# Spreading the spectrum interleave over two phases of the Fourier mixing stage of a two-layer preactivation network

## The chip, the cores and the metric

The kernel runs on one core of a Trainium2 chip. The metric is the device time of one execution in microseconds (us). All data is float32. The engines are named as the profile names them: PE is the matrix engine and PEld its weight load, DVE the vector engine, ACT the scalar engine, POOL the general-purpose engine, SP the engine whose queue issues most of the loads.

## The reference

Input is `x` of 16 images x 16 channels x 256 x 256. Layer 0 normalises `x` in groups and adds a Laplace neural operator; layer 1 is a block of small convolutions, also on a normalised input. Only layer 0's spectral part is touched here:

```python
alpha = jnp.fft.fft2(x, axes=(-2, -1))
A = 1.0 / (omega1[:, None, None, None] - weights_pole1[None])
Bm = 1.0 / (omega2[:, None, None, None] - weights_pole2[None])
S = jnp.einsum('ikpq,oikp,xikq->oxik', weights_residue, A, Bm)
output_residue1 = jnp.einsum('biox,oxik->bkox', alpha, S)
...
x1 = jnp.fft.ifft2(output_residue1, s=(Ny, Nx), axes=(-2, -1)).real
```

For every frequency pair (o, x) a 16 x 16 complex matrix `S[o, x]` over channels is built and multiplied with the spectrum `alpha` of all 16 images; then the inverse transform runs back. Because the input is real, only about half of the o frequencies are computed.

## The kernel before

`forward` runs four stages one after the other: `layer0_forward` (normalisation, forward transform, tables; it leaves the spectrum in the HBM tensor `al`), `layer0_mix` (the stage of this change), `layer0_back` (inverse transform along y, residual) and `layer1`. Inside `layer0_mix` the order of the instructions of PE, ACT, DVE and POOL is the order of the program text (`manual_schedule`); each engine runs its own list in order, and semaphores make it wait where data or buffers need it. The DMAs that SP issues are placed by the scheduler, and SP issues them in that order.

The stage works on 33 groups of four o frequencies (`NF = 33`). For each group g there are two phases.

The **S phase** builds the matrices `S` for group g+1. `residues` (matmuls on line 659) makes eight PSUM tiles per group, two per step f = 0..3; each is copied into the SBUF tile `s` by ACT (line 670) or DVE (line 668). Between them `turn` (line 694) transposes the products `y` of group g, eight transposes per f, each half copied to a tile `yt` by DVE (line 700) and ACT (line 698).

The **mixing phase** has four steps f. Each runs `columns` (line 713), the inverse transform along x of a quarter of the group before, whose two PSUM tiles `ph` are read by ACT (`anti`, line 723) and DVE (`w`, lines 726 and 727) and turned into two tiles `h` by DVE and POOL, which POOL writes to HBM; and then `mix` (line 678), 64 matmul calls of `S` with the spectrum, whose PSUM tile `pg` ACT copies into `y` (line 771).

The spectrum comes to `mix` in three moves. `load_spectrum` (line 607, on SP) loads a piece `alc` of two images, 256 KB; a group has eight pieces, and there are two buffers, so that piece n+2 can be loaded only when piece n has been read. `interleave` copies a piece into the tile `alx` with the image index innermost: DVE copies the even pieces (line 626) and ACT the odd ones (line 624), and it issues the next load. `place` (line 632, on SP) copies `alx` with four DMAs of 512 KB into `alb`, a block-diagonal tile that is zero elsewhere; it can start only when the last `mix` of the group has read the old `alb`.

There is one buffer each of `alx`, `alb`, `y`, `s` and `lt`; two PSUM buffers (tag `pg`) shared by `residues` and `mix`; two each of `pt` and `ph`; four of `yt`; three of `h`. In the text below the eight pieces of a group are called piece 0 to piece 7, and the steps S0 to S3 and M0 to M3. Before the change the pieces are interleaved two per step in M0 to M3, behind the `columns` of the step and ahead of its `y` copy:

```python
ps = mix(s, y, 16 * f)
if more:
    for q in (2 * f, 2 * f + 1):
        interleave(alx, q)
nc.scalar.copy(y[:, :, 16 * f : 16 * f + 16], ps.rearrange("p x j -> p j x"))
```

At the head of the stage `alb` is cleared first, half on DVE and half on POOL (lines 593 and 594), then all eight pieces of group 0 go through the two `alc` buffers, then comes the first S phase, and then the loop over the groups.

Of the kernel before, what the change touches and what calls it, by code (L numbers as in the profile page):

```python
# [10 lines left out]
F32 = mybir.dt.float32  # L11
# [7 lines left out]
C = 16  # L19
N = 256  # L20
G = 8
P = 128
NF = 33
# [542 lines left out]
def layer0_mix(ctx, tc, d, al, hd, tabs):  # L566
# [3 lines left out]
    nc = tc.nc  # L570
    nb = d["x"].shape[0]
# [5 lines left out]
    def load_poles(g):  # L577
        av = ap.tile([P, 32, 4, 3], F32, tag="av", name="av")
        nc.sync.dma_start(out=av.rearrange("p k f l -> p (k f l)"), in_=avd[g])
        return av  # L580

    av = load_poles(0)
# [7 lines left out]


    alb = cp.tile([P, 4, N, nb], F32, name="alb")
    nc.vector.memset(alb[:, :2], 0.0)
    nc.gpsimd.memset(alb[:, 2:], 0.0)

    lp = ctx.enter_context(tc.tile_pool(name="ml", bufs=1))
    gp = ctx.enter_context(tc.tile_pool(name="mg", bufs=1))
    hp = ctx.enter_context(tc.tile_pool(name="mh", bufs=3))
# [4 lines left out]
    def load_spectrum(g, q):  # L603

        t = gp.tile([P, 2, N], F32, tag="alc", name="alc", bufs=2)
        src = al[g // 4 * 2 + g % 2, :, :, :, 2 * q : 2 * q + 2, g % 4 // 2]
        nc.sync.dma_start(out=t, in_=src.rearrange("h v c b x -> (h v c) b x"))
        return t

    wanted = ((g, q) for g in range(NF) for q in range(nb // 2))  # L610
    spectrum = []

    def load_next():

        following = next(wanted, None)
        if following:
            spectrum.append(load_spectrum(*following))

    def interleave(alx, q):

        dst = alx[:, :, 2 * q : 2 * q + 2]
        src = spectrum.pop(0).rearrange("p b x -> p x b")
        if q % 2:
            nc.scalar.copy(dst, src)
        else:
            nc.vector.tensor_copy(dst, src)
        load_next()

    def place(alx):

        for f in range(4):
            nc.sync.dma_start(
                out=alb[f::4, f].rearrange("p x b -> p (x b)"),
                in_=alx[f::4].rearrange("p x b -> p (x b)"),
            )

    def poles(av):


        lt = lp.tile([P, 32, 3, 4, 4], F32, tag="lt", name="lt")  # L640
        shape = [P, 32, 4, 4]
        for plane in range(3):
            nc.vector.tensor_tensor(
                lt[:, :, plane],
                av[:, :, :, plane].unsqueeze(2).to_broadcast(shape),
                m16.unsqueeze(1).unsqueeze(3).to_broadcast(shape),
                ALU.mult,
            )
        return lt.rearrange("p (k g) l c f -> p k g l (c f)", g=4)
# [22 lines left out]
    def mix(s, y, x0):  # L672

        ps = psg.tile([P, 16, 64], F32, tag="pg", name="pg")
        for x in range(16):
            for q in range(4):
                i = 4 * (x0 + x) + q
                nc.tensor.matmul(  # L678
                    ps[32 * q : 32 * q + 32, x],
                    lhsT=s[:, i].rearrange("p v k -> p (v k)"),  # L680
                    rhs=alb[:, :, N // 2 * (i % 2) + i // 2],
                    start=True,
                    stop=True,
                )
        return ps

    def turn(y, f):

        yt = hp.tile([P, 8, 8, C], F32, tag="yt", name="yt", bufs=4)
        for t0 in range(0, 8, 4):  # L690
            pt = pst.tile([P, 4, P], F32, tag="pt", name="pt")
            for t in range(4):
                j = 16 * f + 2 * (t0 + t)
                nc.tensor.transpose(pt[:, t], y[:, j : j + 2].rearrange("p q x -> p (q x)"), ident)  # L694
            dst = yt[:, :, t0 : t0 + 4].rearrange("p c t k -> p t c k")
            src = pt.rearrange("p t (c k) -> p t c k", k=C)
            if t0:
                nc.scalar.copy(dst, src)
            else:
                nc.vector.tensor_copy(dst, src)  # L700
        return yt

    def columns(g, f, yt):

        ph = [psh.tile([P, 2, 4, 64], F32, tag="ph", name="ph") for q in range(2)]
        for e in range(2):
            for v in range(2):
                blocks = slice(0, 4, 3) if v == 0 else slice(1, 3)
                for c in range(2):
                    i = 2 * (2 * c + e) + v  # L710
                    for q in range(2):
                        lanes = slice(64 * q, 64 * q + 64)
                        nc.tensor.matmul(  # L713
                            ph[q][:, e, blocks],
                            lhsT=yt[lanes, i].rearrange("p t k -> p (t k)"),
                            rhs=ix[lanes, i].rearrange("p (b x) -> p b x", b=2),
                            start=c == 0,
                            stop=c == 1,
                        )
        ws = []  # L720
        for q in range(2):
            anti = hp.tile([P, 2, 2, 64], F32, tag="anti", name="anti", bufs=2)
            nc.scalar.copy(anti, ph[q][:, :, 2:])
            w = hp.tile([P, 2, 2, 2, 64], F32, tag="w", name="w", bufs=2)
            sym = ph[q][:, :, :2]
            nc.vector.tensor_tensor(w[:, 0], sym, anti, ALU.add)
            nc.vector.tensor_tensor(w[:, 1, :, :, ::-1], sym, anti, ALU.subtract)  # L727
            ws.append(w)
        for q, w in enumerate(ws):
            o = hp.tile([P, 2, 4, 64], F32, tag="h", name="h", bufs=3)  # L730
            parts = o.rearrange("p v s x -> p s v x")
            nc.vector.tensor_tensor(parts[:, 0::3], w[:, :, 0], w[:, :, 1], ALU.add)
            nc.gpsimd.tensor_tensor(parts[:, 2:0:-1], w[:, :, 0], w[:, :, 1], ALU.subtract)  # L733
            o = o.rearrange("p v s x -> p v (s x)")
            fy = 4 * g + 2 * (f % 2) + f // 2
            if fy % P:
                nc.gpsimd.dma_start(
                    out=hd[fy % 2, :, fy % P // 2, q].rearrange("v b k x -> (b k) v x"), in_=o
                )
            else:  # L740
                nc.gpsimd.dma_start(
                    out=hd[0, fy // P, 0, q].rearrange("b k x -> (b k) x"), in_=o[:, 0]
                )

    E = mybir.EngineType
    with tc.manual_schedule(engines={E.PE, E.Activation, E.DVE, E.Pool}):
        load_next()
        load_next()
        lt = poles(av)
        av = load_poles(1)  # L750
        alx = gp.tile([P, N, nb], F32, tag="alx", name="alx")
        for q in range(nb // 2):
            interleave(alx, q)
        place(alx)
        s = gp.tile([P, N, 2, C], F32, tag="s", name="s")
        for k0 in range(0, C, 2):
            residues(lt, s, k0)
        yts = []
        for g in range(NF):
            more = g + 1 < NF  # L760
            if more:
                alx = gp.tile([P, N, nb], F32, tag="alx", name="alx")
            y = gp.tile([P, 64, 64], F32, tag="y", name="y")
            for f in range(4):
                if g:
                    columns(g - 1, f, yts[f])
                ps = mix(s, y, 16 * f)
                if more:
                    for q in (2 * f, 2 * f + 1):
                        interleave(alx, q)  # L770
                nc.scalar.copy(y[:, :, 16 * f : 16 * f + 16], ps.rearrange("p x j -> p j x"))  # L771
                if more and f == 1:
                    lt = poles(av)
                    if g + 2 < NF:
                        av = load_poles(g + 2)
            yts = []
            if more:
                place(alx)
                s = gp.tile([P, N, 2, C], F32, tag="s", name="s")
                for f in range(4):  # L780
                    for k0 in (4 * f, 4 * f + 2):
                        residues(lt, s, k0)
                    yts.append(turn(y, f))
            else:
                columns(g, 0, turn(y, 0))

# [780 lines left out]
```

## Time and profile before

| what | us |
|---|---|
| median of three runs (lowest, highest) | 6735.75 (6724.75, 6745.13) |
| the profiled execution, its own time | 6730.94 |
| its span in the profile | 6729.2 |
| the mixing stage, first clearing of `alb` to the last `mix` | 1380.0 to about 2556 |
| first `mix` of group 0 | 1420.4 |
| PE busy over the whole span | 6169.1 (92%) |

The span is the stretch from the first to the last instruction in the profile; the profiled execution took 1.7 us more, and was 4.8 us below the median. The stage covers some 17% of the span. A time such as 2087.15 in a line of the profile is a start in us from the span's beginning; the next number is the length. In square brackets stands how long the engine was idle just before, and what ended that idle time; "issue" there means that no semaphore in the profile ended it.

### The profile page before, as it was taken

How to read it: one execution, taken by the hardware profiler on the slowest of the kernel's cores; microseconds unless marked ns; L12 is line 12 of the kernel's file. 1: busy time of each engine (PE TensorE's matmuls, PEld its weight loads, DVE VectorE, ACT ScalarE, POOL GpSimd, SP SyncE). 2: the span in 40 equal slices, each digit the busy share in tenths (PEclk: the TensorE clock that was granted, in tenths of full speed). 3: DMA queues.
4: the chain of work that ended last, by engine and by line, in shares of the span. 5: the costliest groups of instructions: out<-in, count | busy, mean ns of one | idle time of the engine just before them, and what ended most of it. 6: DMA issues, size and time to landing. Idle time of an engine off the chain costs nothing.

```text
span 6729.2 us, 153347 instructions
## 1 busy us (share of the span) xinstructions
PE 6169.1 (92%) x59944; PEld 3412.2 (51%) x59944; DVE 5290.3 (79%) x10118; ACT 3410.0 (51%) x5666; POOL 3531.3 (52%) x4619
## 2 busy tenths in 40 slices
PE   6989989978888888999799999999999999999996
PEld 5777777856777666777233333333333333333331
DVE  8988997535655556888788888888888888888885
ACT  1223333334444442222666666666666666666661
POOL 2334444433333335666556566665667656666563
PEclk9999999989999999999899999999999999999998
DMA  3333433355555558999688888988898888998886
GB/s 98 122 121 124 124 105 118 101 195 188 188 184 189 195 179 279 327 327 316 194 247 256 259 274 268 297 244 265 270 286 277 257 275 268 282 278 258 270 275 213
DMA packets 752372, 1512.38 MB, mean 225 GB/s; under 512 B 82858, under 2 KB 572646, under 8 KB 705286
## 3 DMA queue, kind: packets, MB, share of 16 engines
q1 hardware_dynamic: 623910, 1028.46, 49.3%
q0 software_dynamic: 127744, 474.12, 21.0%
q8 instruction: 478, 7.83, 0.5%
q14 instruction: 240, 1.97, 0.1%
HBM read 876.59 MB, written 556.47 MB: 213 GB/s over the span
## 4 chain that ended last, share of the span: by engine, by line
PE 68%; DVE 16%; DMA 6%; ACT 5%; issue 3%; POOL 1%; SPq 0%; ACTq 0%; DVEq 0%; POOLq 0%
PE c2ps L1207 17%; PE c L1059 14%; PE pd L1127 13%; PE ps L659 4%; PE ph L713 3%; DMA alc<-al 3%; ACT wide L1107 3%; PE pg L678 2%; PE px L313 2%; PE pt L694 2%; DVE u L224 2%; PE py L882 2%; PE pu L207 2%; PE pr L1086 2%; PE py L883 2%
## 5 line engine op out<-in xcount | busy, mean ns | idle before, releaser
L1107 ACT ACTIVATE wide<-c,b 32x512 f32<-32x512 f32 x2176 | 1477.5, 679 | 312.5 <-PE c L1059 264.0
L1138 DVE TENSOR_TENSOR top<-pd,t 32x512 f32<-32x512 f32 x2176 | 1503.9, 691 | 53.9 <-DMA cf<-top 1.3
L1059 PE MATMUL c<-z,w 102*128 102x512 f32 x2048 | 1002.0, 621 | 109.1 <-ACT wide L1107 89.0
L1119 POOL COPY wide<-wide 32x1031 f32<-32x1031 f32 (+1 forms) x576 | 578.6, 1004 | 877.8 <-ACT wide L1107 850.7
L1135 DVE TENSOR_TENSOR t<-pd,r 64x512 f32<-64x512 f32 x1088 | 743.7, 684 | 357.9 <-PE pd L1127 297.0
L1127 PE MATMUL pd<-wide,dw 128*128 128x512 f32 x2048 | 993.9, 607 | 14.8 <-DVE top L1138 11.0
L1207 PE MATMUL c2ps<-rows,c 128*32 128x512 f32 x6144 | 722.9, 603 | 6.3 <-DVE odd L1234 4.8
L1059 PEld LDWEIGHTS c<-z,w 102*128 102x128 f32 x2048 | 373.0, 193 | 697.0 <-issue 462.1
L1127 PEld LDWEIGHTS pd<-wide,dw 128*128 128x128 f32 x2048 | 382.4, 193 | 576.2 <-issue 419.4
L1120 POOL COPY wide<-wide 32x1031 f32<-32x1031 f32 (+1 forms) x576 | 576.8, 1001 | 33.5
L1078 ACT ACTIVATE bot<-c,b 128x512 f32<-128x512 f32 x544 | 344.0, 683 | 468.2 <-issue 384.1
L733 POOL TENSOR_TENSOR h<-w 128x256 f32<-128x256 f32 x258 | 191.5, 742 | 638.4 <-DVE w L727 630.6
L313 PE MATMUL px<-wxn,u 128*64 128x256 f32 x4224 | 481.5, 379 | 4.0 <-ACT o L320 4.0
L207 PE MATMUL pu<-fy,eo 128*128 128x128 f32 x2048 | 432.1, 295 | 48.5 <-DVE u L224 43.9
L1207 PEld LDWEIGHTS c2ps<-rows,c 128*32 128x32 f32 x6144 | 176.9, 109 | 515.6 <-issue 404.3
L895 POOL TENSOR_TENSOR x<-x,o 128x512 f32<-128x512 f32 x256 | 324.0, 1266 | 215.4 <-DVE o L894 215.3
L214 PE MATMUL pv<-at,eo 128*128 128x128 f32 x2048 | 419.4, 288 | 0.0
L313 PEld LDWEIGHTS px<-wxn,u 128*64 128x64 f32 x4224 | 309.1, 137 | 155.2 <-ACT o L320 8.4
L320 ACT ACTIVATE o<-px,rsc 128x512 f32<-128x512 f32 (+1 forms) x272 | 186.1, 686 | 389.2 <-PE px L313 355.5
L194 POOL TENSOR_TENSOR eo<-z 128x1024 f32<-128x1024 f32 x64 | 154.3, 2411 | 401.5 <-PE pv L214 380.9
L207 PEld LDWEIGHTS pu<-fy,eo 128*128 128x128 f32 x2048 | 334.7, 206 | 53.8 <-issue 42.1
L659 PE MATMUL ps<-tt,lt 64*32 64x256 f32 x8448 | 290.8, 402 | 75.6 <-ACT y L771 35.9
(226 smaller groups left out, 11234.7 us busy)
## 6 DMA issues: line engine op xcount, KB each, us to landing
rows<-cf SPq DMA_DIRECT2D x128, 2176.0 KB
z<-zn SPq DMA_DIRECT2D x768, 257.8 KB
cf<-top POOLq DMA_DIRECT2D x512, 240.0 KB, 6.8
cf<-bot POOLq DMA_DIRECT2D x96, 840.0 KB, 11.2
alc<-al SPq DMA_DIRECT2D x264, 256.0 KB
alb<-alx SPq DMA_DIRECT2D x132, 512.0 KB
zn<-zb SPq DMA_DIRECT2D x128, 516.0 KB
o<-zn SPq DMA_DIRECT2D x128, 516.0 KB
```

The lines of the kernel that those rows point to most:

```text
L207: nc.tensor.matmul(pu[:, xh, :, e], lhsT=lhs, rhs=fy[:, e].rearrange("p (v m) -> p v m", v=2), start=True, stop=True,)
L214: nc.tensor.matmul(pv[:, a, xh], lhsT=lhs, rhs=at[:, e, ch].rearrange("p l m -> p (l m)"), start=e == 0, stop=e == 1,)
L313: nc.tensor.matmul(ps[64 * k : 64 * k + 64, :, h], lhsT=u[:, h, part, g0 + j + k].rearrange("p c f g -> p (c f g)"), rhs=wxn[:, h, part], ...
L659: nc.tensor.matmul(ps[32 * g : 32 * g + 32, odd, v], lhsT=lt[lanes, kk, g, 1 - v : 3 - v].rearrange("p l c -> p (l c)"), rhs=tt[lanes, kk, g],
L1059: nc.tensor.matmul(ps[:, a], lhsT=w, rhs=z[:k, c : c + 2, 0:N], start=True, stop=True)
L1107: nc.scalar.activation(self.feat[64 - 32 * q : 96 - 32 * q, f, self.groups[g], :H], ps[q][32 * f : 32 * f + 32], AF.Mish, bias=b1[0][32 * ...
L1119: nc.gpsimd.tensor_copy(flat[0:32, f, 1:m], flat[64:96, f, 0 : m - 1])
L1120: nc.gpsimd.tensor_copy(flat[96:128, f, 0 : m - 1], flat[32:64, f, 1:m])
L1127: nc.tensor.matmul(ps, lhsT=dwt if self.tail else dw, rhs=self.feat[:, f, cs, :H], start=True, stop=True,)
L1135: nc.vector.tensor_tensor(t[64:128], ps[:64], self.r[:, cs], ALU.mult)
L1138: nc.vector.tensor_tensor(self.top[32 * f : 32 * f + 32, cs, q], ps[lanes], t[lanes], ALU.add)
L1207: nc.tensor.matmul(ps[32 * j : 32 * j + 32], lhsT=w[:, blk], rhs=src[:, 4 * j + blk : 4 * j + blk + 4, x : x + H], start=(i, blk) == (0, 0 ...
```

## The change

Four things are done in `layer0_mix`, and one of them at its head.

1. Pieces 0 to 3 of the next group but one are interleaved in the S phase, two each behind the `residues` and `turn` of S2 and the `residues` of S3; pieces 4 to 7 follow in M0 and M1. M2 and M3 have none. The tile `alx` is therefore taken directly after `place` has read the one before.
2. `turn(y, 3)` leaves S3 and stands behind the first `columns` of the next mixing phase, ahead of `mix`.
3. The `y` copy of M3 is written as two halves of 512 columns, the first on ACT and the second on DVE.
4. Group 0's spectrum is loaded by four DMAs of 512 KB into the four `yt` buffers, which are not yet in use; its copies into `alx` come after the first S phase's `residues`. DVE clears its half of `alb` after `poles` and not before it.

```diff
+    def load_first(q):
+        t = hp.tile([P, 8, 8, C], F32, tag="yt", name="first", bufs=4)
+        view = t.rearrange("p t k c -> p (t k c)").rearrange("p (b x) -> p b x", x=N)
+        src = al[0, :, :, :, 4 * q : 4 * q + 4, 0]
+        nc.sync.dma_start(out=view, in_=src.rearrange("h v c b x -> (h v c) b x"))
+        return view
...
-    wanted = ((g, q) for g in range(NF) for q in range(nb // 2))
+    wanted = ((g, q) for g in range(1, NF) for q in range(nb // 2))
...
+        first = [load_first(q) for q in range(nb // 4)]
+        nc.gpsimd.memset(alb[:, 2:], 0.0)
+        lt = poles(av)
+        nc.vector.memset(alb[:, :2], 0.0)
+        av = load_poles(1)
         load_next()
         load_next()
-        lt = poles(av)
-        av = load_poles(1)
-        alx = gp.tile([P, N, nb], F32, tag="alx", name="alx")
-        for q in range(nb // 2):
-            interleave(alx, q)
-        place(alx)
         s = gp.tile([P, N, 2, C], F32, tag="s", name="s")
         for k0 in range(0, C, 2):
             residues(lt, s, k0)
-        yts = []
+        alx = new_spectrum()
+        for q, piece in enumerate(first):
+            copy = nc.scalar.copy if q % 2 else nc.vector.tensor_copy
+            copy(alx[:, :, 4 * q : 4 * q + 4], piece.rearrange("p b x -> p x b"))
+        place(alx)
+        alx = new_spectrum()
+        for q in range(4):
+            interleave(alx, q)
+        yts, last = [], None
         for g in range(NF):
             more = g + 1 < NF
...
             for f in range(4):
                 if g:
                     columns(g - 1, f, yts[f])
+                    if f == 0:
+                        yts.append(turn(last, 3))
+                if f == 0:
+                    y = gp.tile([P, 64, 64], F32, tag="y", name="y")
                 ps = mix(s, y, 16 * f)
-                if more:
-                    for q in (2 * f, 2 * f + 1):
+                if more and f < 2:
+                    for q in (4 + 2 * f, 5 + 2 * f):
                         interleave(alx, q)
-                nc.scalar.copy(y[:, :, 16 * f : 16 * f + 16], ps.rearrange("p x j -> p j x"))
+                dst, src = y[:, :, 16 * f : 16 * f + 16], ps.rearrange("p x j -> p j x")
+                if f < 3:
+                    nc.scalar.copy(dst, src)
+                else:
+                    nc.scalar.copy(dst[:, :32], src[:, :32])
+                    nc.vector.tensor_copy(dst[:, 32:], src[:, 32:])
...
             if more:
                 place(alx)
                 s = gp.tile([P, N, 2, C], F32, tag="s", name="s")
+                if g + 2 < NF:
+                    alx = new_spectrum()
                 for f in range(4):
                     for k0 in (4 * f, 4 * f + 2):
                         residues(lt, s, k0)
-                    yts.append(turn(y, f))
+                    if f < 3:
+                        yts.append(turn(y, f))
+                    if f >= 2 and g + 2 < NF:
+                        for q in (2 * f - 4, 2 * f - 3):
+                            interleave(alx, q)
```

More of the change, by code (lines that the diff above doesn't have):

```diff
@@ L592, in layer0_mix @@
     alb = cp.tile([P, 4, N, nb], F32, name="alb")
-    nc.vector.memset(alb[:, :2], 0.0)
-    nc.gpsimd.memset(alb[:, 2:], 0.0)
     lp = ctx.enter_context(tc.tile_pool(name="ml", bufs=1))
@@ L617, in load_next, with new_spectrum @@
             spectrum.append(load_spectrum(*following))
+    def new_spectrum():
+        return gp.tile([P, N, nb], F32, tag="alx", name="alx")
     def interleave(alx, q):
@@ L757, in layer0_mix @@
             residues(lt, s, k0)
-        yts = []
+        alx = new_spectrum()
[7 more added lines that the diff above has]
+        yts, last = [], None
         for g in range(NF):
             more = g + 1 < NF
-            if more:
-                alx = gp.tile([P, N, nb], F32, tag="alx", name="alx")
-            y = gp.tile([P, 64, 64], F32, tag="y", name="y")
             for f in range(4):
@@ L766, in layer0_mix @@
                     columns(g - 1, f, yts[f])
+                    if f == 0:
+                        yts.append(turn(last, 3))
+                if f == 0:
+                    y = gp.tile([P, 64, 64], F32, tag="y", name="y")
                 ps = mix(s, y, 16 * f)
-                if more:
-                    for q in (2 * f, 2 * f + 1):
+                if more and f < 2:
+                    for q in (4 + 2 * f, 5 + 2 * f):
                         interleave(alx, q)
-                nc.scalar.copy(y[:, :, 16 * f : 16 * f + 16], ps.rearrange("p x j -> p j x"))
+                dst, src = y[:, :, 16 * f : 16 * f + 16], ps.rearrange("p x j -> p j x")
[4 more added lines that the diff above has]
+                    nc.vector.tensor_copy(dst[:, 32:], src[:, 32:])
                 if more and f == 1:
@@ L775, in layer0_mix @@
                         av = load_poles(g + 2)
-            yts = []
+            yts, last = [], y
             if more:
```

## The prediction

> **What bounds the stage now.** I read the page first (PE 92% busy over the span, so a stage that leaves PE idle is where time can be won), then the stretches inside the mixing stage, then the waits in it, then one group in order of time.
>
> From the table of stretches, PE, PEld, DVE, ACT, POOL in turn, then PE's clock, the DMA share and GB/s:
>
> ```profile
> 1452.00:2554.00 1102.00, 954.90 (x29210) 769.62 (x29210) 644.64 (x1227) 488.05 (x752) 372.16 (x508) 0.95 0.56 187
> 2072.00:2074.00 2.00, 2.00 (x48) 1.31 (x40) 1.29 (x2) 1.23 (x2) 0.00 (x0) 1.00 0.83 289
> 2074.00:2076.00 2.00, 2.00 (x61) 1.38 (x46) 0.91 (x2) 1.28 (x2) 0.00 (x0) 1.00 0.08 25
> 2076.00:2078.00 2.00, 2.00 (x31) 1.83 (x31) 1.44 (x2) 0.58 (x1) 0.00 (x0) 1.00 0.00 0
> ```
>
> No engine is full: PE 87%, DVE 58%, ACT 44%. The DMA engines, at 56%, fall to nothing from 2074 to about 2082, late in the S phase. A group's first `y` copy starts at 1452.03 in group 1 and at 2504.68 in group 31, so an inner group takes (2504.68 - 1452.03) / 30 = 35.1 us. PE's own work in one is 27.3 us: four `mix` of 1.93 (2078.45 to 2080.38), four `columns` of 1.98, four S steps of 2.91 (the distance of their transposes). So 7.8 us a group are lost. The waits between 1430 and 2556, who <- whom, sum, times, longest:
>
> ```profile
> ACT alx L624 <- DMA alc<-al: 257.6, 90, 4.7
> PEld ps L659 <- ACT y L771: 50.3, 28, 3.5
> PE pg L678 <- issue: 59.5, 55, 2.8
> PE ph L713 <- issue: 34.7, 23, 2.5
> PE ps L659 <- ACT y L771: 35.9, 17, 3.0
> PE ps L659 <- issue: 10.5, 5, 2.7
> ```
>
> ACT waits 258 us for the spectrum's pieces, and PE's only large semaphore wait is for ACT's `y` copy. One group shows how the two hang together, ACT and then PE:
>
> ```profile
> 2079.13 0.76 ACT L624 COPY alx<-alc 128x512 f32<-128x512 f32 x1
> 2087.15 0.74 ACT L624 COPY alx<-alc 128x512 f32<-128x512 f32 x1 [3.97 <-DMA alc<-al]
> 2092.80 0.75 ACT L624 COPY alx<-alc 128x512 f32<-128x512 f32 x1 [1.43 <-DMA alc<-al]
> 2098.17 0.74 ACT L624 COPY alx<-alc 128x512 f32<-128x512 f32 x1 [2.76 <-DMA alc<-al]
> 2098.82 1.00 ACT L771 COPY y<-pg 128x1024 f32<-128x1024 f32 x1
> ...
> 2086.80 0.41 PE L678 MATMUL pg<-alb,s 128*32 128x64 f32 x11 [2.37 <-issue]
> 2099.87 0.45 PE L659 MATMUL ps<-tt,lt 64*32 64x256 f32 x8 [1.77 <-ACT y L771]
> ```
>
> Pieces 1, 3, 5, 7 end 8.0, 5.6 and 5.4 us apart, because each load can only follow the reading of the piece two before; piece 7 holds the last `y` copy, and that copy holds the second `residues` tile. This chain is one bound: 19.0 us for the pieces, 1.0 for `y`, 10.8 to the end of S3, 2.0 `columns`, 1.4 to the end of piece 1: 34.2 us, as from 2065.6 to 2099.8.
>
> The second bound is in the "issue" rows. In 2086.80 PE stops in the middle of one `mix` of 128 records, where nothing is waited for. These stops sum to 59.5 + 34.7 + 10.5 = 105 us, 3.3 a group. The stage's DMA list has a queue called instruction with 239 transfers, 3.92 MB, 16.4 KB each, in the 1184 us from 1376 to 2560: one in 4.95 us, in which PE and PEld run 2 x 29210 / 1102 x 4.95 = 262 records. I read the stops as instruction blocks that arrive late among the other transfers.
>
> **What the Trainium skill says.** "Runtime: NRT & Kernel Launch", section Instruction fetch mechanics: instructions come in 16 KiB blocks of 256 through a DMA queue of the engine's sequencer. The 262 agree; that the cost is "mostly hidden" does not, with 3.3 us a group. "DMA: Bandwidth & Descriptors", section Issuing engines are not separate DMA queues: all DMAs run on the same 16 engines and interleave, which fits late blocks beside loads. "PSUM — Partial Sum Buffer", section Engine vs sequencer instructions: ACT's and DVE's queues are strict FIFO; the trace agrees, since the `y` copy at 2098.82 follows a piece that waited 2.76 us. "TensorE: Matmul & The Clock Gate", section What's actually happening: the clock halves after an idle window of about 3.4 us; here it was 0.50 from 2088 to 2090 after an idle of only 2.37 us. The mean of 0.95 means a tenth of the time at half clock, 1.7 us a group.
>
> **The change part by part**, for an inner group, counted from the end of the last `mix` (0).
>
> *Pieces 0 to 3 in the S phase.* `place` is issued at 0.1. In the group shown it was issued at 2065.22 and the DMA share collapsed in 2074 to 2076, so it lands 9 to 11 us after; I take 10. The new `alx` copies wait for that, and they stand in ACT's and DVE's queues ahead of the `s` copies of S3 and of all of M0. The last copies of S2's `turn` end at 3 x 2.91 + 0.8 + 0.7 (stall at the start) = 10.2, so this wait is just covered: up to 12.5 it would cost nothing, for S3's two `s` copies are needed only when PE has run `residues` (1.9), `columns` (2.0) and transposes (1.0), at 14.3. Piece 0 (DVE, 0.43) and 1 (ACT, 0.74) are done at 10.7 and 11.0. Loads then run alone on idle DMA engines; in the chain of waits a DMA piece of `alc` is 3.1 to 5.7 us, mostly 4. I take 3.7 here and 4.1 in the mixing phase, where POOL's writes run too. What follows:
>
> - Piece 3 is done at 11.1 + 3.7 + 0.7 = 15.5. Behind it on ACT stand `anti` of M0 (0.65) and the `w` on DVE (1.3 more), so `ph` is free at 17.5; PE, ready at 16.2, runs the second `columns` 17.5 to 19.5.
> - Piece 5 is done at 15.5 + 4.1 + 0.7 = 20.3, then `y` 21.3, `anti` 22.0, `w` 23.3: third `columns` 23.3 to 25.3 (PE ready at 21.5).
> - Piece 7 is done at 25.1, `y` 26.1, `anti` 26.8, `w` 28.1: fourth `columns` to 30.1 (PE ready at 27.3), last `mix` to 32.1.
>
> So the wait in front of the last `y` copy goes, and waits of 1.3, 1.8 and 0.8 us for free `ph` tiles come: 32.1 us a group where no instruction block is late and the clock is full, 3.0 below 35.1. On SP the eight loads now stand ahead of `place`, which waits for PE anyway; POOL's list is unchanged.
>
> *Late blocks and slow clock* are 3.3 + 1.7 = 5.0 us a group, and stay: the same PE instructions run, and eight loads instead of about six now fall between S3 and M3. If all of it lies under the three new waits the group takes 32.1; if none does, 37.1. The two waits and the stops are alike in number and length, so I take half: 34.5, that is -0.6 a group, -19 us for 31 groups. Both ends stay: -93 and +62.
>
> *The last `turn`* moves 1.0 us of PE, and two copies, from S3 to M0, where PE waits for `ph` anyway: 0 (-0.5 to +0.3 a group; inside the sum above).
>
> *The split `y` copy* saves less than nothing. The built program makes DVE's half wait for ACT and not for PE, so that the halves run one after the other: 0.59 + 0.68 (the `yt` copies of the same 128x512) + two handovers of 0.1 = 1.5 instead of 1.0 us. DVE would not be free earlier in any case: its `w` and `h` of M3 end about 0.9 us after the `mix`. PE needs the buffer 0.97 after the `mix`, so the stall is 0.7 instead of 0.3; this 0.7 is in the 10.2 above. If DVE also has to wait for a buffer of `h` it is up to 1.5 more.
>
> *The head.* Before:
>
> ```profile
> 1398.26 0.43 DVE L626 COPY alx<-alc 128x512 f32<-128x512 f32 x1 [9.60 <-DMA alc<-al]
> 1408.43 1.22 DVE L668 COPY s<-ps 128x1024 f32<-128x1024 f32 x1
> 1411.25 3.98 SPq L632 DMA_DIRECT2D alb<-alx  x4
> 1420.44 3.45 PE L678 MATMUL pg<-alb,s 128*32 128x64 f32 x233 [1.73 <-DVE s L668]
> ```
>
> Eight pieces came one by one until 1410, and the `s` copies stood behind them. Now the `residues`, begun at 1388.8, are held only by their table (DMA share 1.0 until 1396) and a half clock, and end near 1402, `s` near 1404. The four loads, issued in place of the two at 1387.96, need 2 MB at some 400 GB/s behind the table: 1402. Two copies an engine (1.3 each on ACT, scaled from 0.74) end near 1406, `place` (9.2, as 1411.25 to 1420.4) near 1415: 5 us earlier. But pieces 1, 3, 5 of group 1 then stand ahead of the first `y` copy, about 10 us of loads, and group 0's S phase, which began near 1433.8, begins near 1431. I take -5 for the head with what group 1 keeps of it (-10 to +4).
>
> Sum: -19 - 5 = -24 on the profiled 6730.94: 6707. That run was 4.8 below the median of the three, so the median goes to 6712.
>
> **Rivals.** About 0.3%, 20 us, is what a measurement of this kernel can tell from no change.
>
> - *Late blocks bound all of it.* With one block in 4.9 us and 7.2 blocks a group, the chain's gain only turns into longer stops. For it: stops in nearly every group. Against: in most groups the last `y` copy starts directly behind piece 7. Only the head remains: 6731.
> - *The chain's gain arrives almost whole*, -2 a group, since PE now stops while it waits for ACT anyway: -62 - 5, 6669.
> - *Slower: the in-order wait.* Piece 3 on ACT blocks everything of M0. Every 0.1 us by which `place` lands later than 10.2, or the S phase's loads take longer than 3.7, lengthens the group by as much, and so does the serial `y` copy. At 3.0 us of delay with stops fully covered, or 0.6 with them half covered, the gain is gone. For it: the pair of loads issued at 2081.62 took to 2087.15, 5.5 us, under light traffic. With 1.8 us more a group it is +1.2: +37 - 5 = +32, 6768.
> - *The change does not do what it says* holds for the split copy, as above, and not for the rest.
>
> **How the numbers follow.** Forecast 0.45 (its own range -45 to -5), blocks bound 0.18, whole gain 0.14, slower 0.23. Of the forecast's 0.45 some 0.27 are beyond 20 us. Faster by over 0.3%: 0.27 + 0.14 = 0.41; within: 0.18 + 0.18 = 0.36; slower: 0.23. The range goes from 6660, below the whole gain, to 6772, about the slower case's middle, which leaves out some 0.17.
>
> **What would show it.** Right: the wait of PE's `residues` for ACT's `y` copy falls from 86 us (PE and PEld) to under 40; a new wait of `columns` on `w` appears, now 8 us, in tens of us; "issue" stops stay near 100 us; ACT's wait for `alc` falls below 258 but not away; `alx` copies in S2 end near the end of `place`; first `mix` near 1415. Wrong: "issue" stops that shrink or grow by half, `s` copies waiting behind `alx` in S3 so that `mix` waits for `s`, or a piece 3 later than 17 us after the last `mix`.

## The result, and the profile after

| | before | after |
|---|---|---|
| median, lowest to highest, us (7 runs each) | 6734.44 (6724.75 to 6745.13) | 6714.8 (6706.67 to 6724.16) |
| ratio of the medians, 95% interval | | 0.997 (0.9959 to 0.9982) |
| the profiled execution, its own time | 6730.94 | 6724.16 |
| its span | 6729.2 | 6722.4 |
| inner group, between the first `y` copies of groups 1 and 31, over 30 | 35.09 | 34.90 |

The change gains 19.6 us, 0.3% (12 to 28 by the interval). The profiled execution of after is the slowest of the seven, 9.4 above their median, and its stage began later: the table of the residues was asked for 11 us later (1390.30 against 1379.17), for the stage ahead of it, which the change doesn't touch, ran longer; so the pair of traces shows where waits went better than how much time was won. In it the stage, from the table's request to the start of the last `mix` instruction, takes 1166.6 us instead of 1175.3, 8.7 less; the stages ahead of it and behind it, the same code in both, differ by 11 and by 9 us.

The waits of the changed kernel from 1430 to 2562: who <- whom, sum in us, times, longest. The residues are line 668 now, `mix` 687, `columns` 722, `alx` 633 (ACT) and 635 (DVE), and the last `y` copy 792 (ACT) and 793 (DVE):

```profile
ACT alx L633 <- DMA alc<-al: 279.7, 96, 4.7
DVE alx L635 <- DMA alc<-al: 58.0, 45, 3.6
PE ph L722 <- DVE w L736: 57.7, 113, 2.1
PE pg L687 <- issue: 38.8, 58, 2.0
PE ps L668 <- issue: 27.9, 31, 1.9
PEld ps L668 <- DVE y L793: 24.8, 28, 1.3
ACT alx L633 <- DMA alb<-alx: 12.8, 11, 1.9
PE ps L668 <- DVE y L793: 11.0, 27, 0.8
PE pt L703 <- issue: 5.2, 4, 2.1
PE ph L722 <- issue: 5.2, 6, 1.5
```

The row of before for the wait on `w`, from 1430 to 2556:

```profile
PE ph L713 <- DVE w L727: 8.0, 26, 0.8
```

Read against before: the residues' wait for the `y` copy fell from 86 to 36 us (PE and PEld together; the two rows overlap in time, and PE alone went from 35.9 to 11.0), the wait of `columns` on `w` rose from 8 to 58, and the "issue" stops of PE fell from 105 to 77. ACT and DVE now wait longer for pieces, not shorter. One wait was exchanged for another: the idle time of PE in these rows is 149 us before and 146 after.

The packets in the traces show what the "issue" stops wait for. From 1430 to 2556 the trace of before has 79 of over 0.2 us, and each of them ends 1.2 to 1.6 us after the end of a 16 KB packet of the queue called instruction; so do all 93 in the trace of after. Of 5000 moments taken at random about 12% lie 1.1 to 1.65 us behind such an end. The stops are waits for instruction blocks, as the prediction read them.

Stretches of the same execution (PE, PEld, DVE, ACT, POOL busy, PE's clock, DMA share, GB/s):

```profile
1464.00:2556.00 1092.00, 945.55 (x29107) 753.96 (x29097) 664.92 (x1252) 465.68 (x750) 376.51 (x504) 0.99 0.59 187
2076.00:2078.00 2.00, 2.00 (x56) 1.55 (x62) 1.73 (x2) 0.62 (x2) 0.34 (x1) 1.00 1.05 344
2080.00:2082.00 2.00, 2.00 (x68) 1.32 (x53) 0.91 (x3) 1.40 (x2) 0.00 (x0) 1.00 1.04 334
2082.00:2084.00 2.00, 2.00 (x63) 1.50 (x68) 1.56 (x2) 0.59 (x1) 0.00 (x0) 1.00 0.35 111
2084.00:2086.00 2.00, 2.00 (x50) 1.59 (x36) 1.57 (x2) 1.74 (x2) 0.00 (x0) 1.00 0.07 13
```

The clock is at 0.99, where it was 0.95, and yet PE is busy for the same share of the stage: 945.55 of 1092 is 86.6%, 954.90 of 1102 was 86.7%. For the same 27840 instructions, from the last `mix` of group 1 to that of group 31, PE is busy for 30.4 us a group before and 30.2 after, and idle for 4.8 and 4.7. The DMA engines carry `place` until about 2083, are idle for some 3 us only, and then carry pieces; before, they idled from 2074 to 2082.

One group in order of time over all engines (start, length, engine; in brackets the idle time before it and what ended it):

```profile
2073.34 0.59 ACT L792 COPY y<-pg 128x512 f32<-128x512 f32 x1 [1.74 <-PE pg L687]
2073.96 0.69 DVE L793 COPY y<-pg 128x512 f32<-128x512 f32 x1 [0.35 <-ACT y L792]
...
2074.71 1.10 PE L668 MATMUL ps<-tt,lt 64*32 64x256 f32 x32 [0.40 <-DVE y L793]
2084.19 0.74 ACT L633 COPY alx<-alc 128x512 f32<-128x512 f32 x1 [0.91 <-DMA alb<-alx]
...
2088.34 0.74 ACT L633 COPY alx<-alc 128x512 f32<-128x512 f32 x1 [2.42 <-DMA alc<-al]
...
2092.41 0.74 ACT L633 COPY alx<-alc 128x512 f32<-128x512 f32 x1 [2.30 <-DMA alc<-al]
...
2097.64 0.74 ACT L633 COPY alx<-alc 128x512 f32<-128x512 f32 x1 [3.03 <-DMA alc<-al]
2101.58 0.46 PE L722 MATMUL ph<-ix,yt 64*128 64x128 f32 x2 [0.80 <-DVE w L736]
```

The halves of the `y` copy run one after the other. The pieces come 10.8 us after `place` was issued (2073.34) and then 4.1, 4.1 and 5.2 apart, each after a wait; PE meets their delay in front of a `columns`.

The head, in the same view:

```profile
1416.88 3.82 SPq L641 DMA_DIRECT2D alb<-alx  x4
1425.46 3.17 PE L687 MATMUL pg<-alb,s 128*32 128x64 f32 x106 [12.15 <-DMA alb<-alx]
...
1434.12 0.74 ACT L633 COPY alx<-alc 128x512 f32<-128x512 f32 x1 [2.81 <-DMA alc<-al]
1434.77 1.00 ACT L790 COPY y<-pg 128x1024 f32<-128x1024 f32 x1
```

Counted from the table's request (1379.17 before, 1390.30 here) the first `mix` starts after 35.2 us instead of 41.3, 6.1 sooner. The second S phase starts after 53.2 instead of 54.6, so 1.4 is kept: piece 5 of group 1 stands ahead of the first `y` copy.

### The profile page after: what moved, and what is told of

It is laid out like the page before. It is cut to its first block, busy times and chain, and to the rows that moved or that the text cites. A ratio compares the mean times of both kernels' runs of the same rounds, so it can differ in the third digit from the quotient of the medians.

```text
span 6722.4 us, 153306 instructions
## 1 busy us (share of the span) xinstructions
PE 6162.6 (92%) x59944; PEld 3403.9 (51%) x59944; DVE 5313.4 (79%) x10149; ACT 3388.8 (50%) x5664; POOL 3542.9 (53%) x4619
## 4 chain that ended last, share of the span: by engine, by line
PE 45%; ACT 3%; DVE 1%; DMA 1%; issue 1%; POOL 1%; SPq 0%; DVEq 0%; POOLq 0%; ACTq 0%
PE c2ps L1235 17%; PE c L1087 14%; PE pd L1155 13%; ACT wide L1135 3%; PE pr L1114 2%; DVE top L1166 0%; POOL o L1303 0%; DMA out_dram<-o 0%; DMA cf<-top 0%; DMA rows<-cf 0%; DVE t L1163 0%; ACT odd L1246 0%; ACT bot L1106 0%; POOL cf L1184 0%; POOL wide L1148 0%
## 5 line engine op out<-in xcount | busy, mean ns | idle before, releaser
L722 PE MATMUL ph<-ix,yt 64*128 64x128 f32 x4128 | 307.2, 283 | 66.1 <-DVE w L736 57.7
```

## The experiments

Twelve kernels ran. The table has them beside the two; "inner group" is worked out from the trace as above, times are medians, and the ratio is to the kernel before on the same chip. A group's length comes from one profiled execution, which can lie 10 us from its kernel's median (the one of after was its slowest, that of e1 its fastest, those of e8, e10 and e11 their slowest); the verdicts go by the medians and ratios.

| kernel | us | ratio, 95% interval | inner group |
|---|---|---|---|
| e4_head_only: before and the head | 6723.8 | 0.9988 (0.9975 to 1.0001) | 35.24 |
| e10_move_only: before and the moved turn | 6706.97 | 0.9963 (0.9950 to 0.9976) | 34.58 |
| e9_m_whole_copy: head and moved turn | 6709.64 | 0.9961 (0.9946 to 0.9976) | 34.39 |
| e2_all_in_m: these and the split copy | 6707.14 | 0.9963 (0.9952 to 0.9974) | 34.57 |
| e3_turn_in_s: changed, turn put back | 6713.72 | 0.9971 (0.9961 to 0.9981) | 34.39 |
| e1_no_split: changed, `y` copy whole | 6701.06 | 0.9951 (0.9933 to 0.9969) | 34.17 |
| e11_y_ahead: e9, `y` of M3 ahead of pieces | 6695.33 | 0.9947 (0.9933 to 0.9962) | 33.93 |
| e7_alc3: e1 with three `alc` buffers | 6676.24 | 0.9920 (0.9903 to 0.9936) | 33.27 |
| e8_alc3_all_in_m: e9 with three | 6676.78 | 0.9909 (0.9892 to 0.9925) | 33.87 |
| e12_alc3_y_ahead: e11 with three | 6668.23 | 0.9913 (0.9898 to 0.9927) | 32.88 |
| e5_after_no_loads | 6633.59 | 0.9848 (0.9828 to 0.9867) | 31.94 |
| e6_before_no_loads | 6612.34 | 0.9816 (0.9796 to 0.9836) | 31.40 |

**The split copy.** e1 writes the `y` copy of M3 as one copy on ACT:

```diff
-                if f < 3:
-                    nc.scalar.copy(dst, src)
-                else:
-                    nc.scalar.copy(dst[:, :32], src[:, :32])
-                    nc.vector.tensor_copy(dst[:, 32:], src[:, 32:])
+                nc.scalar.copy(dst, src)
```

> The changed kernel with the y copy of M3 whole on ACT again. Theory (the two halves run one after the other and hold the second residues tile): PE's wait for that copy, 0.4 us a group in the changed kernel's trace, falls to about 0.3, and the group gets 0.1 to 0.4 us shorter: 3 to 12 us below the changed kernel's 6714.8, about 6707. Rival (late instruction blocks set the pace, so the copy is covered): no difference, 6712 to 6718.

It took 6701.06, 13.7 us less than the change (the theory had 3 to 12), and its slowest run (6705.45) is below the fastest of the changed kernel (6706.67). Its waits from 1430 to 2529:

```profile
PE ph L722 <- DVE w L736: 55.2, 115, 1.5
PE pg L687 <- issue: 33.2, 53, 2.3
PEld ps L668 <- ACT y L789: 16.1, 28, 0.6
```

The wait on `w` is as it was; that of the residues fell from 36 us to 16, and PE itself no longer appears there. In this order of the work, splitting one tile between two engines that take turns lengthened the wait that it should shorten.

**The place of the pieces.** e2 keeps all pieces in M0 to M3 and the other three edits:

```diff
-                if more and f < 2:
-                    for q in (4 + 2 * f, 5 + 2 * f):
+                if more:
+                    for q in (2 * f, 2 * f + 1):
                         interleave(alx, q)
...
-                    if f >= 2 and g + 2 < NF:
-                        for q in (2 * f - 4, 2 * f - 3):
-                            interleave(alx, q)
```

> The changed kernel with all eight pieces interleaved in M0 to M3 again, the other three edits kept. Theory (the interleave in the S phase is what took piece 7 away from the last y copy): PE's wait of residues for the y copy comes back to about 1.1 us a group with stops long enough to slow the clock (some 90 us at half clock in the stage), the inner group goes from 34.9 to about 35.1 us and the time to about 6721 to 6728. Rival (the other edits brought the gain): 6712 to 6718, and the clock stays up.

6707.14: the theory missed. The kernel is no slower without the change's main edit. Its waits from 1430 to 2538:

```profile
PE pg L687 <- issue: 62.3, 53, 2.7
PEld ps L668 <- DVE y L792: 44.5, 29, 3.5
PE ps L668 <- DVE y L792: 30.4, 27, 3.1
PE ph L722 <- issue: 28.5, 23, 2.4
PE ps L668 <- issue: 18.4, 14, 2.7
PE ph L722 <- DVE w L736: 1.2, 6, 0.2
```

The `y` wait is back (75 us), the one on `w` is gone. PE's own idle time for `y`, `w` and instructions (with 1.0 for `pt`) comes to 142 us; in the changed kernel the same rows give 11.0 + 57.7 + 77.1 = 146. With the split copy in both, the main edit moves idle time between causes.

**The last turn.** e3 puts it back into S3 of the changed kernel; e10, later, makes this move alone in the kernel before:

```diff
                     columns(g - 1, f, yts[f])
+                    if f == 0:
+                        yts.append(turn(last, 3))
...
-                    yts.append(turn(y, f))
+                    if f < 3:
+                        yts.append(turn(y, f))
```

> The changed kernel with the last turn back in S3. Theory (in M0 the transposes lie under a wait for ph): no difference or up to 5 us slower, 6712 to 6720. Rival (the shorter S phase is the gain): 1.0 us a group is lost again, 32 us, 6747.

6713.72 against 6714.8: nothing, as expected.

> The kernel before with one edit: the last turn of a group stands behind the next group's first columns. Theory: the kernel with the head alone (6724) and the one with head and turn moved (6710) differ by 14 us, and that is the move: it pays where the pieces lie in M0 to M3, since it takes 1.0 us of PE and two copies out of the S phase, so 6717 to 6724 here. Rival: the move pays nothing, as putting it back into the changed kernel moved nothing (6714 against 6715), and the 14 us are a chance of the measurements or an interplay with the head: 6730 to 6737.

6706.97, 24 us below the kernel before, more than the theory had (6717 to 6724), and as fast as anything that e2, e9 or the whole change reached. Its waits from 1430 to 2554:

```profile
ACT alx L624 <- DMA alc<-al: 218.3, 89, 4.9
PE pg L678 <- issue: 72.9, 60, 3.4
PEld ps L659 <- ACT y L774: 42.3, 28, 3.7
PE ps L659 <- ACT y L774: 27.9, 13, 3.2
PE ph L713 <- DVE w L727: 1.4, 6, 0.3
```

The `y` wait fell from 86 to 70 us, `w` from 8 to 1, ACT's wait for pieces from 258 to 218. The reason lies in the piece chain. Measured from the first `columns` of a mixing phase (means over 28 inner groups of the traces), pieces 1, 3, 5, 7 end at 3.5, 11.2, 16.3, 21.7 us before, and at 4.4, 11.3, 16.4, 21.7 with the turn moved. Piece 1 comes a microsecond later, behind the turn's copies, but piece 3 doesn't. So the M3 copy ends at the same distance (23.1 and 23.4), while the first `columns` itself comes 1.05 us sooner, because the turn has left the S phase. The traces show where the microsecond goes (means over 29 inner groups). SP issues the loads in order, and the one of piece 2 waits until DVE has read piece 0 (5.2 before, 6.2 moved); so the load of piece 3 is issued at 5.7 and 6.7, long after piece 1 was read, and its last packet ends at 10.0 and 10.2. It takes 4.4 us before and 3.5 with the turn moved. Between 7 and 9 POOL's writes of `h` move 334 KB a group beside the two loads before, and 89 KB with the turn moved, where the first write goes out ahead of them. That this traffic is what slows the loads is read from the traces; no run changed it alone.

The change's pieces in S2 and S3 take the early start of the chain in another way, from the end of `place`; then the move has nothing left to give. Read so, the two edits are two cures for the same wait, which fits e2 and e3 together.

**The head.** e4 is the kernel before with the head's edits (four loads of 512 KB, clearing of DVE's half of `alb` later, copies after the residues).

> The kernel before with only the head of the changed one: group 0's spectrum in four loads, copied behind the first residues. Pieces of group 1 are interleaved in M0 to M3 of group 0 as before, so they do not stand ahead of the first y copies. Theory: the first mix comes 6 us earlier, counted from the issue of the tables, as in the changed kernel, and all of it is kept: 6728. Rival (group 1's loads become late instead): 6732 to 6736.

6723.8, 9.3 below its own kernel before, with an interval that just reaches 1. The first `mix` comes 35.1 us after the table's request, the second S phase 51.0 after it: 3.6 sooner than before, so not all of the 6 us is kept, as the theory had it. With e1 and e3, whose heads are those of the change, it is 51.0 and 51.6, so the 53.2 of the trace of after is at the late end.

**Is the split free elsewhere?** e9 is e2 with the whole copy.

> Only the turn's move and the head are kept: all pieces in M0 to M3, the y copy whole on ACT. Against the run with all pieces in M and the split copy (6707) this tells what the split costs where piece 7 stands ahead of the y copy. Theory (the split adds 0.5 us behind piece 7, on the path in most groups): 10 to 16 us faster, 6691 to 6697, which is below the changed kernel without the split (6701), so that moving pieces into the S phase brought nothing. Rival (the split is free there): 6705 to 6710.

6709.64 and 6707.14 are the same, so the theory missed: with the pieces in M0 to M3 the split costs nothing that can be measured, and its price of 14 us belongs to the changed placement. It may also hide a gain of that placement: with the copy whole, the pieces in S2 and S3 (e1, 6701.06) are 8.6 us below all pieces in M0 to M3 (e9, 6709.64). By the ratios (0.9951 and 0.9961, with intervals that overlap) it is 7 us, so a small gain is likely and not shown.

**Without the loads.** e5 and e6 are the changed kernel and the one before with `load_next` taken out of `interleave`, so that every copy reads one of the first two pieces and nearly all of the spectrum is left out:

```diff
-        src = spectrum.pop(0).rearrange("p b x -> p x b")
+        src = spectrum[q % 2].rearrange("p b x -> p x b")
...
-        load_next()
```

> The changed kernel without the loads of the spectrum's pieces: only the first two pieces are loaded, and every copy reads one of these, so the spectrum of groups 1 to 32 is left out; everything else runs. Theory of two bounds (piece chain, and instruction blocks that come late among the loads): waits of ACT and DVE for alc are gone, stops named issue fall well below half of the 70 us, the inner group goes from 34.9 to 29 to 31 us and the time down by 110 to 170 us, to about 6550 to 6600. Rival (instruction blocks come one in 4.8 us whatever else moves): the group stays above 34 us and the time above 6690.

> The kernel before, with the same loads left out in the same way (groups 0 to 32 read the first two pieces). Theory: as there, the inner group falls to 29 to 31 us, and the time to 6560 to 6620, since without the loads the place of the copies hardly matters: within 20 us of the changed kernel without loads. Rival (blocks set the pace): above 34 us a group, above 6700.

6633.59 and 6612.34, from two runs each. The lines move up by one. PE's stops in e6 from 1430 to 2440, with the wait on `w`, and then in e5 from 1430 to 2465:

```profile
PE pg L677 <- issue: 31.6, 39, 1.8
PE ps L658 <- issue: 17.6, 24, 1.4
PE ph L712 <- issue: 7.2, 11, 1.2
PE ph L712 <- DVE w L726: 6.5, 17, 0.8
```

```profile
PE pg L686 <- issue: 38.5, 52, 1.8
PE ps L667 <- issue: 21.7, 28, 2.0
PE ph L721 <- issue: 9.1, 16, 1.2
```

e6 is the upper bound of what earlier pieces can bring: 3.7 us a group in the kernel before (35.09 to 31.40). Little but instruction blocks is waited for there, and the stops fell from 105 us to 57 (with 0.2 for `pt`), although the instruction queue carries the same 16 KB blocks. So in the kernel before about half of the stops go with the pieces' loads, and 1.8 us a group are there without them. In the changed kernel the same removal takes the stops only from 77 us to 71 (with 1.5 for `pt`), so what the loads add depends on the order of the work, and why isn't shown. The packet of a block itself is no longer beside the loads (median 0.97 us in the kernel before, 0.98 in e6); what they add must come before it starts.

Both groups are longer than the theories' 29 to 31 us, 31.40 by a little and 31.94 by these stops and by the split copy's 42 (PE and PEld). The time of e6 lies in its range, that of e5 33 us above its. Between the two, the changed order is 21 us the slower one where no load has to be hidden.

**The chain loosened.** A third `alc` buffer, first with all pieces in M0 to M3 (e8), then in the changed placement with the whole copy (e7):

```diff
-        t = gp.tile([P, 2, N], F32, tag="alc", name="alc", bufs=2)
+        t = gp.tile([P, 2, N], F32, tag="alc", name="alc", bufs=3)
...
-        load_next()
-        load_next()
+        for _ in range(3):
+            load_next()
```

> All pieces in M0 to M3, the y copy whole on ACT, the turn and the head as in the changed kernel, and three alc buffers in place of two, so that three loads are under way. Theory (the piece chain is one of two bounds): ACT's wait for alc falls from some 260 us to under 120, the group to 33 us or less, the time to about 6650 to 6670. Rival (late blocks bound it, and three loads together delay them more): no gain over the same kernel with two buffers, 6690 to 6710.

> The changed kernel with the y copy of M3 whole and three alc buffers. Theory: the S-phase half of the interleave brings nothing with three buffers either, so the time is that of the kernel with all pieces in M0 to M3 and three buffers (6677): 6672 to 6688, with the wait of alx for alc well under half of 280 us. Rival: early pieces and three buffers together free M0 to M3 of load waits: 6650 to 6668.

6676.78 and 6676.24: 33 and 25 us below the same kernels with two buffers, the largest step of the study, and the two times are the same, so the placement is worth nothing where three loads can be under way. The time of e7 is the one that the theory gave; the gain of e8 is a little smaller than the theory had it (6650 to 6670).

> Head and moved turn, all pieces in M0 to M3, and the y copy of M3 whole on ACT but ahead of pieces 6 and 7 instead of behind them. Theory: the piece chain ends in that copy and holds the next group's residues (33 us of PE's idle time in the same kernel with the copy behind); without that hold the wait goes and the group is 0.5 to 0.9 us shorter: 6680 to 6695. Rival: late instruction blocks, or place, which now waits for pieces 6 and 7 alone, take the time over: 6705 to 6714, with the wait for y gone and another in its place.

```diff
+                if f == 3:
+                    nc.scalar.copy(dst, src)
                 if more:
                     for q in (2 * f, 2 * f + 1):
                         interleave(alx, q)
-                nc.scalar.copy(dst, src)
+                if f < 3:
+                    nc.scalar.copy(dst, src)
```

6695.33, just outside the theory's range and 14 us below e9: the `y` copy of M3 ended 22.4 us after the first `columns` (23.4 in e9), piece 7 at 23.4 (21.7). From 1430 to 2400 the rows of the residues' wait for `y` fell from 28.3 on PE and 41.6 on PEld in e9 to 13.6 on PEld alone, and no `mix` waits for `place`. By the ratios to each one's own kernel before (0.9947, 0.9961) the gain is 9 us, so its size is less sure than its sign: the slowest run of e11 (6702.37) is below the fastest of e9 (6705.46). ACT's queue is strictly in order ("PSUM — Partial Sum Buffer" of the Trainium skill, section Engine vs sequencer instructions, says so, and the copy at 2098.82 of the kernel before shows it), so the order of two copies in the text was enough.

> Head and moved turn, all pieces in M0 to M3, three alc buffers (6677 with the y copy of M3 behind piece 7) and that y copy ahead of pieces 6 and 7. Theory: with three buffers pieces 6 and 7 still sometimes come late, so the copy ahead of them is worth a part of the 14 us that it brought with two buffers: 6663 to 6673. Rival: with three buffers piece 7 is in time and the order is worth nothing: 6674 to 6682.

6668.23. The theory's range held it, but against their own kernels before it stands at -63 and e8 at -59, with ratios of 0.9913 and 0.9909: the two can't be told apart. Its waits from 1430 to 2488:

```profile
ACT alx L633 <- DMA alc<-al: 64.6, 49, 2.6
PE pg L687 <- issue: 63.3, 57, 2.7
PE ph L722 <- issue: 25.3, 22, 2.5
PE ps L668 <- issue: 12.2, 13, 2.5
PE ph L722 <- DVE w L736: 1.9, 8, 0.3
```

Of PE's large waits only those for instruction blocks are left, 102 us with 0.8 for `pt`: of the two bounds that the prediction named, the second is what PE still stops for. e7, e8 and e12 beat both kernels.

## Why the prediction was right, step by step

The forecast was -24 for the median and the result is -19.6, in the likeliest case's own range. Its parts did not all come out as they were priced, and that the sum lies within 5 us of the result is in part luck: the pieces came late and the clock gave less than was charged to it, while the blocks stopped PE less.

- **Two bounds, the piece chain and the late blocks: right.** Taking the loads away opens 3.7 us a group, and loosening the chain (e8, e12) leaves little but "issue" stops. One link of the chain is finer than the prediction had it: the load of piece 3 waits, on SP, for the one of piece 2, and so for DVE's reading of piece 0 and not for ACT's of piece 1.
- **Pieces in the S phase: right in kind, late by one to two microseconds.** Pieces 1, 3, 5, 7 were put at 11.0, 15.5, 20.3 and 25.1 us after the last `mix`; means over the inner groups of the trace of after are 12.4, 17.2, 21.4 and 26.7. `place` took 10.8 in the group shown (10 was taken) and the first copies queue behind others. Piece 3, at 17.2, is past the 17 that the prediction gave as a sign of being wrong (16.8 in e1, 16.7 in e3, so at its edge). The intervals in the sum were nearly right: 4.8, 4.2, 5.3 for 4.5, 4.8, 4.8.
- **One wait for another: right.** The `y` wait fell to 36 us, PE and PEld together (under 40 was said), the wait on `w` rose to 58 ("tens of us").
- **Late blocks stay near 100 us: off.** They fell to 77. The stops in `mix` and `columns` fell from 94 to 44 and those in the S phase, where the loads now fall, rose from 10.5 to 33. That PE's new waits on `w` hide the arriving blocks is argued, not shown; in e5, where these waits are 4 us and no loads run, the stops are 71.
- **ACT's wait for pieces falls below 258: wrong.** It rose to 280, and 58 on DVE came with it. Pieces read as early as possible are waited for in full; this says nothing of PE.
- **Half of the late blocks and slow clock lies under the new waits, -0.6 a group: about right in sum, unsafe in reason.** The clock did recover (0.95 to 0.99), but of the 1.7 us a group that the prediction charged to it PE's busy time fell by only 0.2.
- **The last turn at 0: right where it was priced, in the changed kernel (e3).** That it was worth 24 us in the kernel before (e10), without any other edit, was not seen: the step looked only at PE, which waits for `ph` anyway, and not at when the chain starts.
- **The split copy loses: right.** 0.7 instead of 0.3 us a group was in the sum, 12 us over 31 groups; 13.7 was measured.
- **The head at -5: right within its bounds.** Counted from the table's request the first `mix` is 6.1 sooner, where 5 was forecast; alone the head gave 9.3, with an interval from a loss of 1 to a gain of 17.

The rivals: the blocks bounding all of it (6731) and the whole chain gain (6669) are out by the interval of the ratio, and so is the slower one (6768). Its mechanism, the in-order wait behind a late piece 3, is there: the delay of 1.7 us lies between the 0.6 and the 3.0 that the prediction named as the points where the gain is gone, and in the profiled pair the inner group gained only 0.2 us, where the forecast has 0.6; in e3, whose median is that of the change, it gained 0.7, so one trace of each does not tell the size.

The change's sum from the experiments: head -4 (its trace) to -9 (its median); then either the moved turn or the pieces in the S phase, some -20 each when alone and at most 9 more together; then +14 for the split copy. The pieces in the S phase without the moved turn and without the split were not run; that they would be worth some 24 is an estimate from e3, e4 and the price of the split.

## What to carry to other kernels

When two edits shorten the same chain, each can be worth nearly the whole gain alone and little beside the other: undo one at a time, and also do one at a time. A copy that the next phase needs shouldn't stand, on an in-order engine, behind copies that wait for loads, and where the loads are the chain, one more buffer (25 to 33 us) beat a cleverer place for their readers (some 7 to 9 us with two buffers, not clear of noise, and nothing with three). Two engines that took turns on one tile cost 14 us here where no late piece stood ahead of the copy (e1), and nothing where pieces 6 and 7 did (e2 and e9).

## What was not expected of the hardware

- PE's clock rose from 0.95 to 0.99 over the stage and PE's busy share stayed at 86.6%. e10 won as much as the whole change with a clock of 0.97 (1470 to 2480). A recovered clock was no gain by itself. What recovered it was the length of the stops and not their sum: idle times of PE of 1.8 us or more, from 1450 to 2556, went from 38 to 5, and stretches at half clock from 28 (102 us) to 6 (21 us), while the idle time a group stayed at 4.8 and 4.7 us. In before each of the 28 begins between 0.6 us ahead of the end of an idle time of 1.85 to 2.96 us and 1.7 us behind it, but 10 idle times of 1.8 us or more, one of 3.0 among them, brought none; in after four of the six go with idle times of 0.8 to 1.5 us.
- Instruction blocks stop PE for 1.8 us a group in the kernel before without the pieces' loads (57 us in e6), and for 3.3 with them. A stop ends 1.2 to 1.6 us after the block's packet does.
- A load of 256 KB is carried in 272 packets, 256 of 1024 bytes and 16 of 4 bytes: of 1024 bytes, queue q1 has 67584 packets in the stage of before with 264 such loads and 512 with the 2 of e6; of 4 bytes, 6976 and 2784.
